# A memset between two scatters of GpSimd, one word wide or 320 columns on all partitions

## The chip, the cores and the metric

The kernel runs on one core of a Trainium2 chip. The core has five engines that work side by side, each in the order of its own instructions: PE (matrix products), DVE (VectorE), ACT (ScalarE), POOL (GpSimd) and SP (which here only issues transfers). They wait for one another through semaphores. The metric is device time in microseconds. Before the change it is 736.45 us, the median of three runs (736.4 to 737.74).

## The reference

The input x holds 64 sequences of 128 tokens with 128 features, the context 64 sequences of 77 tokens with 96 features. A gated cross-attention with 16 heads is followed by a gated mixture of 8 experts, of which each token takes its two best:

```python
x = x + tanh(g_xattn[0]) * xattn(layernorm(x), ctx_768, mask, Wq, Wk, Wv, Wo)
x = x + tanh(g_ffn[0]) * ffn(layernorm(x), Wg, W11, W12, W2)
# xattn: softmax(q k^T * 8**-0.5) v per head, then Wo
# ffn:   top 2 of softmax(x Wg), scores divided by their sum;
#        per expert (silu(x W11) * (x W12)) W2; weighted sum of the two
```

The reference computes all experts for all tokens and then picks. The kernel sends each token only to its two experts.

## The kernel before

The 64 sequences are worked in 16 groups of four (G = 4). The kernel has three stages.

**Attention and gating** (lines 268 to 758). One loop runs over the 64 sequences. In turn i it computes the scores of sequence i, transposes and exponentiates those of i-1 and mixes the values of i-2. The work that belongs to a whole group is cut into small functions, each registered with `step(dt)`: the function runs for group g in turn 4g + dt, after the turn's attention (or ahead of it, with PRE). `advance` (line 731) calls what is due, over the groups in order. So turn i carries steps of several groups, and steps whose numbers differ by four fall into the same turn. The order on PE, ACT, DVE and POOL is exactly the order in which the code issues instructions (`manual_schedule`, line 279): no engine overtakes its own queue. Steps reach up to 30, so the loop goes on for some 25 turns after the attention of the last sequence.

The steps that matter here use POOL. The first layer norm has its factors on POOL (`factors`, lines 305 to 311, in steps -13), and so has the selection matrix `sel` (steps -14 to -12). After the attention of a group, the second layer norm has its factors on POOL (step 13). The token numbers are written by an iota (line 497, step 15), the normed rows are copied a second time (line 506, step 16), the chosen experts are turned into one-hot form (`took`, lines 555 to 569, step 22), and the counts per expert are kept up (`both` and `run`, lines 573 to 578, step 23). PE turns the counts into places (`pp`, lines 584 and 585, step 24), POOL picks the places (`at`, line 597, step 25), DVE sums them (`to`, line 604) and POOL casts them to integers (`dest`, line 606, step 26).

Then the tokens are dispatched. Steps 27 to 30 call `dispatch(b)` for the four sequences of the group. Each issues two indirect transfers from the queue of POOL, which write the 128 rows of a sequence (132 words each) to the places of their first and second expert in the DRAM buffer `xg`. After each of them POOL clears the tile `spare_w`:

```python
i = nc.gpsimd.indirect_dma_start(
    out=xg[:, :],
    out_offset=bass.IndirectOffsetOnAxis(ap=gr.dest[:, k, b : b + 1], axis=0),
    in_=gr.rows[:, b, k, :], in_offset=None,
)
apart(i, "dispatch")
nc.gpsimd.memset(spare_w, 0.0)
```

Nothing reads `spare_w`. There are 64 x 2 = 128 scatters and as many memsets. The scatters are declared to touch rows of their own, so they don't wait for one another.

**Expert tiles** (lines 761 to 898). The counts give a table of 135 tiles of 128 rows (lines 766 to 803). SP fills the unused rows with empty ones (lines 805 to 812) and loads one tile after another (`load`, line 831), which needs all scatters to have landed. PE multiplies with the expert's weights (lines 851 and 874), and POOL scatters each result to `yb` (line 881).

**Sum** (lines 901 to 919). The two results of each token are loaded, weighted, added to x and stored.

Of the kernel before, what the change touches and what calls it, by code (L numbers as in the profile page):

```python
# [8 lines left out]
F32 = mybir.dt.float32  # L9
# [25 lines left out]
def tile_gated_xattn_moe(  # L35
# [21 lines left out]
    P = 128  # L57
# [14 lines left out]
    const = ctx.enter_context(tc.tile_pool(name="const", bufs=1))  # L72
# [181 lines left out]
    czs = [const.tile([CD, G, 3, JL], F32, name=f"czs{i}") for i in range(3)]  # L254
    for t in pls + czs:
        nc.gpsimd.memset(t, 0.0)
    spare_w = const.tile([1, 1], F32, name="spare_w")

    wt = keep.tile([P, NG, G, TOPK], F32, name="wt")

# [692 lines left out]
```

## Time and profile before

| what | us |
|---|---|
| median of three runs | 736.45 |
| profiled execution, its own time | 771.93 |
| its span | 770.0 |
| POOL busy in the span | 420.9 |
| scatters of the tokens, L611, 128 of them | 129.2 |
| memsets of `spare_w`, L620, 128 of them | 11.3 |
| first and last scatter of the tokens start at | 166.4 and 489.9 |
| attention, one group before and after the scatters begin | 21.3 and 26.1 |
| expert tiles, from about 501 to 723 | 222 |

The profile shows one execution, taken by the hardware profiler, and it took longer than the runs without it. Its parts are the busy time of each engine, the same over 40 slices of the span, the chain of work that ended last, and groups of instructions by line. In a group's row stand the line, the engine, the operation, what it writes and reads, how often, then the busy time in us, the mean of one in ns, and the idle time of the engine ahead of it with what ended that idle time. A timeline row begins with start and length in us; the value in brackets is the idle time ahead, with what ended it. A row of waits gives total, number of times and longest. "issue" is time in which an engine waited for nothing that the profile shows.

### The profile page before, as it was taken

The numbers are of one execution on the slowest core, as the hardware profiler recorded it, in microseconds if no ns is written. First come the engines' busy times: TensorE is split into PE (matmuls) and PEld (weight loads), VectorE is DVE, ScalarE is ACT, GpSimd is POOL, SyncE is SP. The second block draws the span as 40 slices with busy tenths as digits, with TensorE's granted clock in tenths as the row PEclk, the third lists the DMA queues.
The fourth block names the chain that finished last, engine by engine and source line by source line (L and its number), as shares of the span: only waits on it lengthen the run. The fifth ranks groups of instructions, "written<-read, shape, count | busy, mean of one in ns | idle before, by whom it ended". The sixth has DMA issues, their size and how long they took to land.

```text
span 770.0 us, 21086 instructions
## 1 busy us (share of the span) xinstructions
PE 610.8 (79%) x7626; PEld 439.4 (57%) x7626; DVE 473.5 (61%) x1446; ACT 363.9 (47%) x881; POOL 420.9 (55%) x792
## 2 busy tenths in 40 slices
PE   2999999999999889999983220299999999999400
PEld 1677777776676666776762120166666666666300
DVE  4567888987677777677864113155544554555297
ACT  1678787776666666677542100043443344434100
POOL 5411133356767676755668888445665556555400
PEclk9999999999999999999995555599999999999755
DMA  6841111111211111011112011222222222222299
GB/s 184 212 118 30 29 29 29 23 22 43 50 43 32 38 38 38 25 39 46 39 46 49 32 39 60 70 63 82 81 82 82 80 81 83 75 84 81 65 323 289
DMA packets 86948, 56.86 MB, mean 74 GB/s; under 512 B 15773, under 2 KB 82738, under 8 KB 86848
## 3 DMA queue, kind: packets, MB, share of 16 engines
q1 hardware_dynamic: 68512, 33.78, 18.7%
q0 software_dynamic: 8416, 17.06, 6.7%
q10 hardware_dynamic: 9920, 4.69, 2.1%
q8 instruction: 62, 1.02, 0.5%
q14 instruction: 38, 0.31, 0.1%
HBM read 28.50 MB, written 22.73 MB: 67 GB/s over the span
## 4 chain that ended last, share of the span: by engine, by line
PE 68%; POOL 11%; ACT 6%; issue 5%; DMA 4%; DVE 3%; SPq 1%; POOLq 0%; ACTq 0%; DVEq 0%
PE pu L851 14%; PE po L717 13%; PE pot L874 7%; PE tp L685 7%; POOL xg L611 7%; PE sc L663 5%; PE phh L866 4%; PE tl L698 3%; PE pv L638 2%; DVE x L913 2%; ACT kb L421 2%; DMA ys<-yb 2%; PE pq L432 2%; PE ptt L841 2%; PE py L470 2%
## 5 line engine op out<-in xcount | busy, mean ns | idle before, releaser
L881 POOL DMA_INDIRECT yb<-y,xt x135 | 132.6, 982 | 102.2 <-DVE xTt L843 83.8
L611 POOL DMA_INDIRECT xg<-rows,dest x128 | 129.2, 1010 | 24.9 <-issue 24.9
L851 PE MATMUL pu<-wx,xTt 128*128 x270 | 140.3, 601 | 0.8 <-DVE xTt L843 0.5
L672 DVE TENSOR_REDUCE mx<-sc 128x16 f32<-128x1232 f32 x64 | 92.3, 1442 | 66.2 <-PE sc L663 65.2
L859 DVE TENSOR_TENSOR ht<-sgt,pu 128x256 f32<-128x256 f32 x135 | 56.8, 421 | 96.1 <-issue 80.7
L857 ACT ACTIVATE sgt<-pu 128x256 f32<-128x256 f32 x135 | 51.8, 384 | 130.1 <-PE pu L851 96.4
L690 ACT ACTIVATE pT<-tp,drop 128x512 f32<-128x512 f32 x128 | 81.9, 688 | 42.2 <-PE tp L685 41.2
L874 PE MATMUL pot<-wx,hTt 128*128 x540 | 82.4, 275 | 0.1
L675 DVE TENSOR_TENSOR pe<-sc,mx 128x1024 f32<-128x1024 f32 x64 | 78.4, 1224 | 2.2
L866 PEld LDWEIGHTS phh<-ident,ht 128*128 128x128 f32 x270 | 38.0, 141 | 70.1 <-issue 67.4
L874 PEld LDWEIGHTS pot<-wx,hTt 128*128 128x128 f32 x540 | 70.8, 191 | 0.5 <-DVE y L880 0.3
L685 PEld LDWEIGHTS tp<-ident,pe 128*128 128x128 f32 x512 | 55.5, 142 | 26.8 <-issue 14.7
L685 PE MATMUL tp<-ident,pe 128*128 128x128 f32 x512 | 70.8, 282 | 0.0
L717 PE MATMUL po<-pT,va 128*32 128x128 f32 x1536 | 64.5, 275 | 6.8 <-issue 4.3
L717 PE MATMUL po<-pT,own 128*32 128x128 f32 x1536 | 65.1, 273 | 5.0 <-issue 4.8
L654 ACT COPY va<-pv 128x384 f32<-128x384 f32 x64 | 30.8, 481 | 52.7 <-PE po L717 40.2
L841 PE MATMUL ptt<-ident,xt 128*128 128x128 f32 x135 | 37.5, 278 | 22.4 <-DMA xt<-xg 22.0
L717 PEld LDWEIGHTS po<-pT,own 128*32 128x32 f32 x1536 | 47.7, 110 | 10.8 <-issue 10.4
L663 PE MATMUL sc<-kb,qT 32*128 32x308 f32 x512 | 52.5, 480 | 0.0
L866 PE MATMUL phh<-ident,ht 128*128 128x128 f32 x270 | 51.6, 273 | 0.0
L717 PEld LDWEIGHTS po<-pT,va 128*32 128x32 f32 x1536 | 41.5, 110 | 15.4 <-issue 11.7
L868 ACT COPY hTt<-phh 128x256 f32<-128x256 f32 x135 | 49.5, 368 | 1.4 <-PE pot L874 0.7
(158 smaller groups left out, 1063.8 us busy)
## 6 DMA issues: line engine op xcount, KB each, us to landing
xt<-xg SPq DMA_DIRECT2D x135, 66.0 KB
ys<-yb SPq DMA_DIRECT2D x32, 256.0 KB
rb<-rz SPq DMA_DIRECT2D x64, 64.0 KB
out_dram<-x ACTq DMA_DIRECT2D x16, 256.0 KB
x<-in_x_dram SPq DMA_DIRECT2D x15, 256.0 KB
yb<-y,xt POOLq DMA_INDIRECT x135
wx<-in_L_ffn_W_dram SPq DMA_DIRECT2D x2, 1024.0 KB
xg<-rows,dest POOLq DMA_INDIRECT x128
```

Source lines behind the costliest of these rows:

```text
L611: i = nc.gpsimd.indirect_dma_start(out=xg[:, :], out_offset=bass.IndirectOffsetOnAxis(ap=gr.dest[:, k, b : b + 1], axis=0), in_=gr.rows[:, ...
L663: nc.tensor.matmul(sc[:, q, :W], gr.qT[r, b * S : (b + 1) * S], gr.kb[r, b].rearrange("p h j -> p (h j)"), start=True, stop=True,)
L672: nc.vector.tensor_reduce(mx[:, :, :, 0], sv, AX.X, ALU.max)
L675: nc.vector.tensor_tensor(dst[:, :, :, : j1 - j0], sv[:, :, :, j0:j1], mx.to_broadcast([P, NQ, HQ, j1 - j0]), ALU.subtract,)
L685: nc.tensor.transpose(tp[:, u, :], pe[:, q + u // 2, 2 * (u % 2) : 2 * (u % 2) + 2].rearrange("p h j -> p (h j)"), ident,)
L690: nc.scalar.activation(pT[:, 2 * q : 2 * q + 4], tp, AF.Exp, bias=drop[:, 0, i : i + 1], scale=scale)
L717: nc.tensor.matmul(po[32 * q : 32 * q + 32, v, :], w, pT[:, 2 * q + c if c < 2 else 8 + q // 2, :], start=(c == 0), stop=(c == 2),)
L851: nc.tensor.matmul(pu.rearrange("p j i -> p (j i)"), ti.xT, wxf[:, bass.ds(ti.e, 2 * I)], start=True, stop=True,)
L859: nc.vector.tensor_tensor(ti.h.rearrange("p c i -> p (c i)"), sg, pu[:, 1], ALU.mult)
L866: nc.tensor.transpose(pt[:, c], ti.h[:, c], ident)
L874: nc.tensor.matmul(po, ti.hT[:, c], wxf[:, bass.ds(ti.e + w, D)], start=(c == 0), stop=(c == NC - 1),)
L881: i = nc.gpsimd.indirect_dma_start(out=yb[:, :], out_offset=bass.IndirectOffsetOnAxis(ap=ti.x[:, D : D + 1].bitcast(I32), axis=0), in_=y, ...
```

## The change

The tile `spare_w` gets 320 columns on all 128 partitions, where it was one word on one partition. The memset in `dispatch` is written for the whole tile, so it now fills 128 x 320 words each of its 128 times. Order, waits and transfers are as they were.

```diff
-    spare_w = const.tile([1, 1], F32, name="spare_w")
+    spare_w = const.tile([P, 320], F32, name="spare_w")
```

## The prediction

> **What bounds the kernel now.** I read the page's busy table and slices first. No engine bounds the whole span, so it has to be cut into stages.
>
> ```profile
> PE 610.8 (79%) x7626; PEld 439.4 (57%) x7626; DVE 473.5 (61%) x1446; ACT 363.9 (47%) x881; POOL 420.9 (55%) x792
> ...
> PE   2999999999999889999983220299999999999400
> ...
> POOL 5411133356767676755668888445665556555400
> ```
>
> The reader is to see the dip of PE to 2 or 3 tenths in the slices from 400 to 490 us, where POOL stands at 8. I cut the span there and asked for the stages: one group of the attention with scatters running, the dip, and the expert tiles (columns: stage, length, then busy time and count of PE, PEld, DVE, ACT, POOL).
>
> ```profile
> 269.00:295.00 26.00, 23.76 (x401) 17.38 (x401) 19.50 (x56) 16.91 (x39) 17.81 (x40) 1.00 0.15 35
> 399.20:491.00 91.80, 20.05 (x102) 16.83 (x94) 26.26 (x144) 8.57 (x21) 78.31 (x183) 0.53 0.16 47
> 501.00:723.00 222.00, 219.53 (x1207) 148.69 (x1206) 111.40 (x402) 87.42 (x269) 130.39 (x133) 1.00 0.27 78
> ```
>
> The expert stage belongs to PE (219.5 of 222) and has no spare_w memset. In the dip POOL is busy 78.3 of 91.8 us, and nearly all the rest is the 10.4 us marked "issue" ahead of its 52 scatters plus gaps below 0.2 us. The waits of that stage say who is late:
>
> ```profile
> PEld pp L584 <- POOL both L575: 42.0, 4, 12.1
> POOL rows L506 <- ACT rows L321: 2.7, 1, 2.7
> ```
>
> POOL waits for another engine once, at 399.1, and after that the others wait for it. The chain that ended last runs over POOL from 399.14 to the last scatter (489.95), then its landing (2.34), SP's loads of xt and the first expert tile. So what POOL does between 399 and 490 sets the end.
>
> Then the POOL timeline within the dip and, in a second fence, the rows of the memsets (groups by shape: busy, mean ns, idle before):
>
> ```profile
> 427.04 0.09 POOL L620 MEMSET spare_w<- 1x1 f32 x1
> 427.10 0.25 POOL L575 TENSOR_TENSOR both<-took 128x32 f32<-128x32 f32 x1
> 427.43 1.03 POOL L578 TENSOR_TENSOR run<-run,both 128x8 f32<-128x8 f32 x4
> 428.41 0.27 POOL L497 IOTA rows<- 128x16 int32 x2
> 428.84 0.98 POOL L611 DMA_INDIRECT xg<-rows,dest  x1 [0.16 <-issue]
> 429.83 0.09 POOL L620 MEMSET spare_w<- 1x1 f32 x1
> 430.13 0.97 POOL L611 DMA_INDIRECT xg<-rows,dest  x1 [0.21 <-issue]
> ```
>
> ```profile
> L620 POOL MEMSET spare_w<- 1x1 f32 x128 | 11.3, 88 | 0.3
> L256 POOL MEMSET pls<- 128x256 f32 x3 | 0.8, 301 | 0.0
> L256 POOL MEMSET czs<- 96x192 f32 x3 | 0.6, 248 | 0.0
> ```
>
> POOL's instructions follow one another here without waiting for anyone.
>
> [...] from 192 to 256 columns 301 - 248 = 53 ns, 0.83 ns a column. [...] Spacing here confirms the slope: three memsets of 256 columns take 0.76 us (4.09 to 4.85), three of 192 take 0.60 (4.85 to 5.45), so 0.253 and 0.200 each, again 0.83 ns a column. [...]
>
> **The change part by part.** Nothing is removed, added or moved: 128 memsets keep their places and their waits, and each writes 320 columns of 128 partitions in place of one word. Price: 88 ns now; 301 + 64 x 0.83 = 354 ns after. That is 266 ns more, and 319 x 0.83 = 265 by the spacing. Can this hide in the gap ahead of the next scatter? From the predecessor's end to the scatter's end it takes 0.21 + 0.96 = 1.17 us after today's memset, 1.14 after the iota (428.68 to 429.82), 1.16 after the copy L506 (0.61 long). The length of the predecessor adds in full, and at most 0.03 of the gap goes. I take 0.01 off for the 31 memsets or so of the dip that stand directly before a scatter.
>
> *In the dip*: 52 memsets start from 401.2 to 490.9. The last has no scatter behind it, so 51 count: 51 x 0.266 = 13.6, less 31 x 0.01 = 0.3, gives 13.3 us on the path. Bounds: 12.6 if 0.03 goes each time, 13.6 if nothing goes.
>
> *Before the dip*: 76 memsets, 20.2 us of POOL work. What hides it is POOL's idle time, here in the group at 269 us:
>
> ```profile
> 275.38 0.24 POOL L307 TENSOR_SCALAR ve_a<-mv_a 128x4 f32<-128x4 f32 x1 [0.87 <-DVE mv_a L303]
> ...
> 282.80 0.61 POOL L506 COPY rows<-rows 128x512 f32<-128x512 f32 x1 [2.37 <-ACT rows L321]
> ...
> 287.66 0.69 POOL L307 TENSOR_SCALAR ve_f<-mv_f 128x4 f32<-128x4 f32 x1 [0.76 <-DVE mv_f L303]
> ...
> 293.57 0.19 POOL L606 CAST dest<-to 128x8 int32<-128x8 f32 x1 [1.44 <-DVE to L604]
> ```
>
> There are four steps to a group, two memsets to a step (0.53 us), and each step ends in a wait of at least 0.76, so POOL arrives later and still waits. One step, at 382.43, has only 0.38; 0.15 us carries over into the next wait of 0.79, which still leaves 0.11. Queued behind the memsets are both and run (PE's pp L584 waits for them), at (VectorE's to L604), and the rest of the next scatter. They come 0.3 to 0.5 us later; both ends at 348.03 where pp starts at 354.88, so about 6.9 us lie between. Cost: nothing, and the 20.2 us in full if that cover is gone. The ready counts let SP's empty rows go out well before the last scatter, which stays so.
>
> Everything behind the last scatter moves by the same amount: landing, loads, expert tiles, sum. The tile takes 1276 bytes more of each partition; I set this to nothing.
>
> Sum for the profiled execution: 771.93 + 13.3 = 785.2 (span 770.0 to 783.3). The median of the runs is 736.45, 35.5 us below its own profile, and I add the same 13.3 there: **749.8 us**, +1.8%. The dip consists of POOL's own work and its memsets are fixed by the order of steps, so I expect its share to be alike in both. What may differ is the cover: a group takes 21.3 us before the scatters start and 26.1 after (six groups, 4.8 x 6 = 29 us), and if the unprofiled runs lack that stretching, POOL's spare 5.9 us a group fall to 1.1 while the memsets ask for 2.1. That leaves it 1.0 us late per group, 6 us in all by 321 us. Behind that, POOL has 5 to 7 us idle in each group of this trace and can catch up, and pp's 6.9 us of slack takes such a lag. So 0 to 6 us may come on top, up to 756.
>
> **The rivals.**
> *The cover fails.* POOL becomes the bound already in the attention. For it: the 35.5 us above. Against: the four waits shown. In part, 752 to 757; in full, 736.45 + 13.3 + 20.2 = 770.
> *Part is absorbed.* [...] less than the 0.266 counts. Half gives 743. [...] Against: iota and copy add in full.
> *Not slower.* The scatter's 0.96 us could hold a wait [...], and a longer memset would stand in that wait. It decides if that wait is 0.266 or more in every scatter of the dip; then the time stays at 736.5. For: three scatters of the dip take 1.24, 1.31 and 1.65 us, together 1.3 us above the usual. Against: the expert stage's scatters (L881), with 0.6 us of idle ahead of each, take 982 ns, no less than the 960 of two scatters that stand close. Shorter than before would need the three outliers and more.
>
> **How the numbers follow.** The dip alone (748 to 751.5): 0.63. Some of the attention as well (751.5 to 757): 0.17; beyond 757: 0.06. Partly absorbed (738 to 748): 0.10. Not slower: 0.04. About 0.2% (1.5 us) is what a measurement of this kernel can tell from no change. The range 746 to 757 holds the first two and a little of the absorbed case, some 0.82. Faster 0.02, same 0.03, slower 0.95.
>
> **What would show it.** The row of L620 at about 354 ns x128; POOL's stretch from the last wait for ACT to the last scatter at some 104 us in place of 90.8; 52 memsets still in it; groups at 26 us as before; POOL's four waits per group shorter by about half a microsecond each; expert stage 222 us. Wrong if the groups of the attention grow (the cover), if scatters behind the memset get shorter (the absorbed wait), or if L620 reads well off 354 ns.

## The result and the profile after

The changed kernel takes 750.58 us (median of four runs, 750.0 to 751.12), the kernel before 736.42 beside it (four runs, 736.13 to 737.74). The ratio is 1.0181, with a 95% interval from 1.0162 to 1.0200: 14.2 us or 1.8% slower, against 13.3 us predicted.

One thing has to be said first, or the two profiles contradict each other. The profiled execution of the changed kernel has a span of 749.1 us and fits its runs. The one shown of the kernel before had 770.0 us, 35 more than the runs of that kernel. A repeat of the kernel before (run e0 below) left a profile with a span of 734.9 us, and all comparisons here are with that one. The experiments ran on three chips. On that of e0 to e3 the kernel before takes 737 us; on that of e4 to e8 and on that of e9 and ea it takes 772 us in every run. So the first profile shows something real, only not what the timed runs did.

The stages of the changed kernel: one group of the attention with scatters, the stretch from POOL's 13th copy of rows to the last scatter, and the expert tiles (columns as before: stage, length, busy time of PE, PEld, DVE, ACT, POOL, then clock and DMA).

```profile
229.50:251.22 21.72, 21.53 (x401) 16.75 (x402) 19.18 (x56) 16.83 (x39) 19.51 (x41) 1.00 0.18 42
366.29:470.12 103.83, 19.06 (x82) 16.28 (x82) 26.23 (x143) 7.71 (x20) 91.89 (x183) 0.52 0.14 41
481.00:702.30 221.30, 218.99 (x1206) 148.67 (x1206) 110.27 (x402) 87.21 (x269) 130.59 (x133) 1.00 0.29 78
```

The same three stages in the repeat of the kernel before:

```profile
228.60:250.30 21.70, 21.50 (x400) 16.61 (x400) 18.93 (x52) 16.56 (x38) 17.63 (x38) 1.00 0.18 42
365.07:455.68 90.61, 20.01 (x102) 16.79 (x90) 26.19 (x143) 8.57 (x21) 77.12 (x182) 0.53 0.16 48
466.50:688.00 221.50, 219.60 (x1208) 148.51 (x1206) 110.38 (x402) 87.61 (x270) 130.66 (x133) 1.00 0.27 78
```

A group of the attention lasts the same 21.7 us in both, with POOL busy 19.5 instead of 17.6 us. The expert stage hasn't moved. The middle stage is 13.2 us longer. In it POOL waits for no other engine; the rows of its waits in the changed kernel, from 348.6 us on, are:

```profile
POOL xg L611 <- issue: 9.9, 59, 0.2
POOL xg L611 <- POOL dest L606: 0.3, 1, 0.3
```

The rows of the memset and of the scatters in the changed kernel (groups by shape; one line's instructions with shortest, median and longest in ns, and the first and last start):

```profile
L620 POOL MEMSET spare_w<- 128x320 f32 x128 | 49.1, 384 | 0.3
```

```profile
L611 POOL DMA_INDIRECT xg<-rows,dest x128: 964/980/1433, 166.4 to 470.1; - x128
```

And the scatters of the repeat of the kernel before:

```profile
L611 POOL DMA_INDIRECT xg<-rows,dest x128: 954/973/1646, 165.9 to 455.7; - x128
```

A scatter takes as long as it did, 980 ns in the median against 973. The last one starts 14.4 us later, and the span is 14.2 us longer: all of the loss lies ahead of the last scatter.

How the memset stands among its neighbours is seen in the timeline of POOL. First the changed kernel:

```profile
245.07 0.97 POOL L611 DMA_INDIRECT xg<-rows,dest  x1 [0.17 <-issue]
246.03 0.39 POOL L620 MEMSET spare_w<- 128x320 f32 x1
246.36 0.33 POOL L597 TENSOR_TENSOR at<-took,place 128x64 f32<-128x64 f32 x1
```

Then the same place in the repeat of the kernel before:

```profile
265.51 0.97 POOL L611 DMA_INDIRECT xg<-rows,dest  x1 [0.21 <-issue]
266.47 0.09 POOL L620 MEMSET spare_w<- 1x1 f32 x1
266.52 0.34 POOL L597 TENSOR_TENSOR at<-took,place 128x64 f32<-128x64 f32 x1
267.41 0.69 POOL L307 TENSOR_SCALAR ve_f<-mv_f 128x4 f32<-128x4 f32 x1 [0.55 <-DVE mv_f L303]
```

The memset's row reads 384 - 88 = 296 ns more. But from its start to the start of `at` it is 0.33 against 0.05 us, so 0.28 more; and where a scatter follows, from the memset's start to the scatter's end, it is 1.52 (244.52 to 246.04) against 1.27 (265.21 to 266.48), so 0.25 more, because the gap ahead of the scatter shrinks from 0.21 to 0.17. The mean of the two is the 0.265 of 319 columns, and the middle stage is longer by 13.2 us for 51 memsets, 0.259 each. So the spacing tells what a memset cost here, and the 296 ns of its row are too many.

### The profile page after: what moved, and what is told of

Same layout as the page of the kernel before. It is cut to its first block, busy times and chain, and to the rows that moved or that the text cites. A ratio compares the mean times of both kernels' runs of the same rounds, so it can differ in the third digit from the quotient of the medians.

```text
span 749.1 us, 21086 instructions
## 1 busy us (share of the span) xinstructions
PE 592.0 (79%) x7626; PEld 434.4 (58%) x7626; DVE 470.5 (63%) x1446; ACT 362.6 (48%) x881; POOL 454.0 (61%) x792
## 4 chain that ended last, share of the span: by engine, by line
PE 68%; POOL 15%; ACT 5%; issue 4%; DVE 3%; DMA 3%; SPq 1%; POOLq 0%; ACTq 0%; DVEq 0%
PE pu L851 15%; PE po L717 11%; POOL xg L611 8%; PE pot L874 8%; PE tp L685 7%; PE sc L663 5%; PE phh L866 4%; DVE x L913 3%; POOL spare_w L620 3%; PE pv L638 3%; PE tl L698 2%; PE pq L432 2%; ACT kb L421 2%; PE ptt L841 2%; PE pv L648 2%
## 5 line engine op out<-in xcount | busy, mean ns | idle before, releaser
L611 POOL DMA_INDIRECT xg<-rows,dest x128 | 129.4, 1011 | 21.7 <-issue 21.4
L717 PE MATMUL po<-pT,va 128*32 128x128 f32 x1536 | 54.2, 274 | 2.0 <-ACT kb L421 1.5
L584 PE MATMUL pp<-both,earlier 128*128 128x32 f32 x32 | 6.6, 290 | 61.4 <-POOL both L575 61.4
L717 PE MATMUL po<-pT,own 128*32 128x128 f32 x1536 | 53.7, 273 | 0.0
L620 POOL MEMSET spare_w<- 128x320 f32 x128 | 49.1, 384 | 0.3
L843 DVE COPY xTt<-ptt 128x128 f32<-128x128 f32 x135 | 37.9, 281 | 16.2 <-PE ptt L841 16.2
```

The source lines that it names most:

```text
L611: i = nc.gpsimd.indirect_dma_start(out=xg[:, :], out_offset=bass.IndirectOffsetOnAxis(ap=gr.dest[:, k, b : b + 1], axis=0), in_=gr.rows[:, ...
L717: nc.tensor.matmul(po[32 * q : 32 * q + 32, v, :], w, pT[:, 2 * q + c if c < 2 else 8 + q // 2, :], start=(c == 0), stop=(c == 2),)
```

## The experiments

**e0, the kernel before once more.** No edit.

> The kernel before, unchanged, for a profile of an execution that takes what the runs take. Both theories: 736.4 us, ratio 1.000. If the profiled execution shown ahead of the prediction (771.9 us) was stretched in the attention, then here a group with scatters takes about 21.7 us as it does in the changed kernel's profile, not 26.1, and POOL is idle about 2 us in a group (21.7 less the some 19.6 us of its own work). The dip from the last wait of POOL to the last scatter should then start with 52 to 60 scatters still to come, and the last scatter should start at about 456 us. If instead the stretching lies elsewhere, the groups stay at 26.

Measured: 736.93 us, ratio 1.0002 (0.9995 to 1.0009). The groups last 21.7 us. POOL's waits in one group:

```profile
250.31 0.19 POOL L606 CAST dest<-to 128x8 int32<-128x8 f32 x1 [0.19 <-DVE to L604]
250.86 0.19 POOL L556 CAST ki<-i 128x8 f32<-128x8 uint32 x1 [0.35 <-DVE gt L551]
...
257.74 0.24 POOL L307 TENSOR_SCALAR ve_a<-mv_a 128x4 f32<-128x4 f32 x1 [0.45 <-DVE mv_a L303]
```

With the 0.55 at 267.41 above that is 1.5 us in a group, and one of the four waits of the first profile, that for the rows, is gone until 306 us. The eight memsets of a group ask for 2.1 us. So in an execution that takes what the timed ones take, the recorded waits are too short to cover them. The last scatter starts at 455.7, as expected.

**e1 and e2, one half each.** A second tile keeps the one-word memset:

```diff
-                    nc.gpsimd.memset(spare_w, 0.0)
+                    nc.gpsimd.memset(spare_w if G * g + 27 + b >= 65 else spare_n, 0.0)  # e1
+                    nc.gpsimd.memset(spare_n if G * g + 27 + b >= 65 else spare_w, 0.0)  # e2
```

> The 320-column memset only in the scatter steps that fall after the last attention turn (52 of the 128), one word in the others. Theory (only the memsets that POOL runs with no wait left count): nearly the whole loss, +13.3 us, 749.7. Rival (the cover in the attention fails as well and the loss is spread over all 128): 52/128 of 14.2, +5.8 us, 742.2.

> The other half: 320 columns in the first 76 memsets, one word in the 52 after the attention. Theory: POOL's waits hide them, +0 to 2 us, 736.4 to 738.4. Rival (spread evenly): +8.4 us, 744.8. POOL's idle time in a group should be close to zero here, and the last scatter should start where it does in the kernel before, or up to 2 us later.

Measured: e1 750.45 us, 13.4 more than the 737.04 of the kernel before beside it (ratio 1.0183, 1.0157 to 1.0210); e2 738.14, 1.1 more (1.0019, 1.0009 to 1.0028). The two add up to the 14.2 of the whole change, within their intervals. Fewer than half of the memsets carry over nine tenths of the cost. An even spread is refuted twice, by 5.8 against 13.4 and by 8.4 against 1.1. The last scatters confirm it; first e1, then e2:

```profile
L612 POOL DMA_INDIRECT xg<-rows,dest x128: 954/976/1430, 166.3 to 468.7; - x128
```

```profile
L612 POOL DMA_INDIRECT xg<-rows,dest x128: 954/980/1645, 165.8 to 456.7; - x128
```

**e3 and e4, other widths.** The tile is `[P, 640]` and `[P, 160]`.

> 640 columns in all 128 memsets: 0.267 us more on each than in the changed kernel. Theory: in the changed kernel's profile POOL hardly waits any more in the attention, so the second 320 columns are hidden nowhere: 127 x 0.267 = 33.9 us on top of 750.6, 784.5, and less than that only by the some 4 us that POOL still waits. Rival (cover as good as for the first 320): 14.2 more, 764.8.

> 160 columns in all 128 memsets. Theory (0.83 ns a column, only the memsets after the attention count): 159 x 0.83 = 0.132 us each, 51 of them 6.7 us, and in the attention POOL's waits hide 8 x 0.132 = 1.1 us a group altogether: 737.0 + 6.7 = 743.7. Rival (a fixed price for a memset that is not a single word): the same 13.5 as with 320 columns, 750.5.

Measured: e3 778.42 us, 41.4 more than before (ratio 1.0556, 1.0527 to 1.0585), so 27.2 on top of the first 14.2. The direction is the theory's: the second 320 columns cost almost twice as much as the first. The size is 6 us short of 784.5. The expectation set the waits left in the changed kernel at some 4 us; counted afterwards, from the first scatter to 348.6 us in its profile, they are 5.7 for the rows and 1.1 for ve_f, 6.9 in all, and 33.9 - 6.9 = 27.0. In e3 the attention itself has become longer, 24.3 us a group (the casts of `dest` start at 236.78 and 261.05), and PE waits for `both` there (2.1 us in four waits from 190 to 330 us).

e4 ran on the second chip, where the kernel before takes 772.28 beside it: 777.63, ratio 1.0088 (1.0060 to 1.0115). That is 6.8 us by the ratio and 5.4 by the medians, where the theory had 6.7. A fixed price for any memset beyond a word would have given 13.5, which lies outside the interval (4.6 to 8.9). The rows of the two widths, e3 and then e4:

```profile
L620 POOL MEMSET spare_w<- 128x640 f32 x128 | 83.3, 650 | 0.3
```

```profile
L620 POOL MEMSET spare_w<- 128x160 f32 x128 | 32.1, 251 | 0.3
```

From 160 to 640 columns the row grows by 399 ns, 0.83 a column.

**e6 and e7, what of the fill costs.** In e6 the tile is `[1, 320]`; in e7 it is `[P, 320]`, but the memset fills `spare_w[:1, :1]`. Both ran on the second chip, too, beside 772.28 us.

> The memset fills 320 columns of one partition only. Theory (the columns cost[...]): as 128 partitions, 750.5. Rival (the number of words [...] costs): close to the kernel before, 737 to 738.

> The tile is 128 x 320, but the memset fills one word of it. Separates the fill from the 1276 bytes a partition by which the later tiles move. Theory: 737.0, ratio 1.000. Rival (the moved tiles cost or gain): anything beyond 1.5 us.

Measured: e6 ratio 1.0170 (1.0136 to 1.0203), 13.1 us more by the ratio; e7 ratio 0.9995 (0.9981 to 1.0009). The large tile costs nothing that can be measured. 320 words in one partition cost as much as 40,960 words in all, within the intervals (13.1 us against 14.2), so in these runs columns are what is paid for. The row of e6:

```profile
L620 POOL MEMSET spare_w<- 1x320 f32 x128 | 45.3, 354 | 0.2
```

354 ns is the price that the prediction had worked out for 320 columns. What refutes the rival by which only part of that price counts is the middle stage above, where 51 memsets take 13.2 us more, 0.259 each.

**ea, the changed kernel beside the kernel before on the third chip.** No edit.

> The changed kernel again, beside the other. On a chip where the kernel before takes about 772 us, its groups with scatters take 26 us and POOL waits 5.9 us in each, so the attention should hide its share in full: +13.2 us, ratio 1.017. On one where it takes about 737 us, POOL waits only some 1.7 us a group: +14.4 us, ratio 1.019 to 1.020. Rival (no difference between the two in what is hidden): 14.2 us on either.

Measured: 783.77 against 771.79, ratio 1.0147 (1.0104 to 1.0190), 11.3 us by the ratio and 12.0 by the medians. The interval reaches from 8 to 15 us and so holds 13.2 as well as 14.2: it doesn't tell the two apart. The price of the stretch after the attention is the same there: from the 13th copy of rows (397.06 us) to the last scatter (501.24) it is 104.2 us, against 90.8 in the first profile of the kernel before (399.14 to 489.95).

**e8 and e9, a kernel in which POOL has less to do after the attention.** In the steps that fall into turn 65 or later, `ki`, `took`, `gt`, `wt`, `both`, `run`, `at`, `dest` and the second copy of the rows move to VectorE:

```diff
+        def free(g, dt):
+            return nc.vector if G * g + dt >= 65 else nc.gpsimd
...
-                nc.gpsimd.tensor_tensor(run[:, i + 1], run[:, i], gr.both[:, b], ALU.add)
+                free(g, 23).tensor_tensor(run[:, i + 1], run[:, i], gr.both[:, b], ALU.add)
```

(the others alike). e8 keeps the one-word memset, e9 has 128 x 320.

> Starts from the kernel before, one-word memset. In the steps that fall after the last attention turn (turn 65 on) the small operations took, gt, wt, both, run, at, dest and the second copy of the rows move from POOL to VectorE, which is idle there for some 70% of the time; POOL keeps the scatters, the memsets, the iotas and the factors of the norm. Theory (POOL's own work after the attention sets the end): in the repeat of the kernel before, POOL takes 90.6 us from its last wait to the last scatter; 52 scatters with their memsets at 1.24 us make 64.5, the factors and iotas some 6, so up to 20 us go: 717 to 722. Rival (the chain of counts and places through PE and VectorE sets the end as soon as POOL is faster): half of it or less, 727 to 735.

> The kernel in which VectorE takes POOL's small work after the attention, now with the 320-column memset. There the chain that ended last ran over SP's writes of empty rows and no longer over POOL. Theory (a memset counts only from where POOL is late): 51 x 0.26 = 13.3 us less the some 3.5 us by which POOL is early there, so about 10 us more than with one word, ratio to the kernel before about 0.983 + 0.013 = 0.996. Rival (the price of a memset counts wherever it stands): 13.3 to 14.2 more, ratio 1.001 to 1.002.

Measured: e8 758.17 against 772.28, ratio 0.9833 (0.9803 to 0.9864): faster than the kernel before on the second chip by 12.9 us by the ratio, 14.1 by the medians. Both forecasts missed: it is less than the theory's 15 to 20 us and more than the rival's half. The timeline of POOL in e8 shows what is left:

```profile
430.13 0.96 POOL L614 DMA_INDIRECT xg<-rows,dest  x1 [0.21 <-issue]
431.08 0.09 POOL L623 MEMSET spare_w<- 1x1 f32 x1
431.39 0.96 POOL L614 DMA_INDIRECT xg<-rows,dest  x1 [0.23 <-issue]
432.34 0.09 POOL L623 MEMSET spare_w<- 1x1 f32 x1
432.39 0.29 POOL L500 IOTA rows<- 128x16 int32 x2
```

Two scatters with a memset between follow one another after 1.26 us. From the 13th copy of rows (398.87) to the last scatter (471.81) it is 72.9 us, 17.9 less than in the first profile. Some 3.6 us are given back behind it: 755.5 - 471.8 = 283.7 us to the end, against 770.0 - 489.9 = 280.1. The chain that ended last explains that. It can be followed back to 473.4 us, and from there on it runs over SP and holds no scatter:

```profile
473.45 0.70 issue
474.14 0.70 SPq L812
474.84 0.01 issue
474.86 0.69 SPq L812
...
476.76 1.61 DMA xg<-empty
```

The last of SP's writes of empty rows starts at 476.76, after the last scatter, and SP's loads begin when it has landed (478.4). So in e8 these writes end the stage. But there SP is also slow: from the landing that it last waited for (473.44) to the start of the last write it takes 3.3 us, where eight of these writes take 8.7 us in the first profile (474.23 to 482.90), 1.1 each. Why it is slow there was not found.

e9, on the third chip: 770.09 against 771.79, ratio 0.9973 (0.9953 to 0.9994). From 0.9833 to 0.9973 is 0.0140 of 772, 10.8 us, as the theory had it. That agreement is luck, since its mechanism is not in the profile. In e9 the chain that ended last runs over POOL's scatters and memsets from 445.29 us to the last memset (483.49) and holds no write of empty rows, so POOL isn't early against these. And a second thing changed beside the memset. The iota `tn` (line 790), for which the table of expert tiles on VectorE waits, stands outside the part with a fixed order. In all other timelines 24 scatters are still to come behind it (it starts at 440.20 in e8); in e9 it stands behind them all. POOL, then VectorE:

```profile
482.52 0.96 POOL L614 DMA_INDIRECT xg<-rows,dest  x1 [0.17 <-issue]
483.49 0.38 POOL L623 MEMSET spare_w<- 128x320 f32 x1
483.81 0.28 POOL L790 IOTA tn<- 128x135 f32 x1
```

```profile
484.12 1.28 DVE L795 TENSOR_TENSOR ge__7381<-tn,after 128x1080 f32<-128x1080 f32 x1 [35.05 <-POOL tn L790]
```

The table is ready only at 490.6, and SP's loads of tiles begin behind it, at 490.59. From the last scatter to the end it is 769.5 - 482.5 = 287.0 us, against 283.7 in e8 and 279.3 in e7 (769.5 - 490.2). The last scatter itself starts 10.7 us after that of e8. So e8 and e9 don't measure what the wide memset costs where something else is later than POOL. They ran on different chips besides, and the two intervals together leave some 8 to 13.6 us for the difference, which holds the rival's 13.3. The theory's claim stays unproven.

## Why the prediction was right, and where not

**The price of a memset**: predicted 266 ns, less 10 before a scatter. Right by the spacing (0.25 and 0.28). The prediction also said that the row would read 354. It reads 384, and exactly 354 with one partition (e6). The rows of 128-partition memsets in the scatter steps lie 30 ns above what the memsets at the kernel's start gave. Little of that shows in the spacing: from the start of a memset to the end of the scatter behind it the median after the attention is 1.51 us in the changed kernel and 1.27 in the repeat, 0.24 more.

**51 memsets in the dip, 13.3 us**: right, and for the reason given. 103.8 - 90.6 = 13.2 in the profiles, and 13.4 in e1. The larger tile at nothing was right as well (e7).

**76 memsets before the dip at nothing**: wrong by 1.1 us, and for a reason that the prediction had seen from far off. It read the cover from an execution whose groups took 26.1 us, with waits of at least 0.76 at four places of a group. In the repeat, which takes what the timed runs take, a group takes 21.7 us and POOL's waits in it come to 1.5 to 1.7. So the argument of the four waits failed, and the prediction's second case (groups at 21.3, 1.1 us of spare, 0 to 6 us on top) was the true one, at its lower end.

That it came out at the lower end is in part luck. The memsets of a group ask for 2.1 us and the waits hold 1.6, but a row changed too: `ve_f` takes 0.69 us where it has waited and 0.23 to 0.26 where it hasn't, but for one case with 0.69 and no recorded wait (351.91 in the changed kernel). The next row starts that much sooner. Why the row changes was not found. Here first the repeat of the kernel before, then the changed kernel:

```profile
223.74 0.69 POOL L307 TENSOR_SCALAR ve_f<-mv_f 128x4 f32<-128x4 f32 x1 [0.63 <-DVE mv_f L303]
```

```profile
224.94 0.23 POOL L307 TENSOR_SCALAR ve_f<-mv_f 128x4 f32<-128x4 f32 x1
```

1.6 and 0.46 make the 2.1 us. From 176.66 to 285.46 us, five groups, POOL in the changed kernel doesn't wait for another engine even once, and each group still takes 21.7 to 21.8 us. The cover was used up to the last, and the prediction had not counted on that row.

The group ahead of these five is 0.8 us longer than before, which goes into the wait of the 10th copy of rows. From there on POOL waits for the rows again, and the 12th copy of rows starts at 347.96 before and 347.93 after. The loss arises in the eight memsets between that copy and the 13th, 17.1 us before and 18.4 after. The halves agree: it is 17.1 in e1 and 18.4 in e2. The views of the place:

The repeat of the kernel before:

```profile
347.96 0.61 POOL L506 COPY rows<-rows 128x512 f32<-128x512 f32 x1 [2.52 <-ACT rows L321]
...
351.94 0.70 POOL L307 TENSOR_SCALAR ve_f<-mv_f 128x4 f32<-128x4 f32 x1 [0.56 <-DVE mv_f L303]
...
365.07 0.61 POOL L506 COPY rows<-rows 128x512 f32<-128x512 f32 x1 [0.30 <-ACT rows L321]
```

The changed kernel:

```profile
347.93 0.61 POOL L506 COPY rows<-rows 128x512 f32<-128x512 f32 x1 [1.43 <-ACT rows L321]
...
366.29 0.97 POOL L506 COPY rows<-rows 128x512 f32<-128x512 f32 x1
```

Eight memsets ask for 2.1 us, and the two waits between hold 0.86; the rest is the 1.25 us. The prediction had marked this place as the thinnest (a wait of 0.38 with 0.11 left over behind it), but in the stretched execution it just held.

**The rivals.** Cover failing in full (770): refuted by e2, but e3 shows where it begins, since at 640 columns the attention pays too. Part absorbed: refuted by the 13.2 us of the dip and by e1 (13.4); e4 and e6 agree (6.8 and 13.1 by the ratio). Not slower, if a scatter's row held a wait that a longer memset would fill: refuted, as its median is 973 ns before and 980 after. Of the long scatters of the dip (1.30 and 1.65 us in the repeat) one stays (1.43), which is worth about half a microsecond.

**What was to be seen**: the stretch at some 104 us (103.8), the expert stage unmoved (221.3). "Groups at 26 as before" held only in so far as they are as before; they are at 21.7. POOL's waits in a group, which were to be shorter by half a microsecond each, are gone altogether in five groups.

Left open: how the 1.1 us would stand on the chips with 772 us, where POOL has more spare time in the attention (5.8 us of recorded waits in a group of e7, 205.44 to 231.43 us, against 1.5 in the repeat). ea doesn't resolve it.

## What to carry to other kernels

Here an instruction that "does nothing" cost its time where its engine ran without a wait (13.4 us for the memsets after the attention, e1), so count the instances in that stretch and multiply by the spacing. The others were nearly free (1.1 us, e2) until the cover was used up, and then they cost as well, as most of the second 320 columns did (27.2 of 33.9 us, e3). The cover is not only the waits that a profile records: a row that waited can itself be longer, as `ve_f` was by 0.46 us here. Before reading small covers of half a microsecond off a profile, compare the profiled execution's own time with the runs: here they differed by 5%, and the waits in it were not those of the timed runs. Where one engine drains a queue alone while another idles, moving small work across can be worth as much as trimming the fill (e8, 12.9 us). And before two runs are compared, look whether the edit moved something else, as it moved `tn` in e9.

## What was not expected of the hardware

The same program takes 737 us on one chip (734.8 to 739.0 in 39 runs) and 772 on two others (769.2 to 774.9 in 24 runs, 770.2 to 773.8 in 15). The runs of each chip lie close together in time, so that it is the chip that makes the difference isn't shown. The difference lies in the attention while scatters run, and for the most part in the products of the mixing: both halves of them, with the idle time ahead of them, account for 28 of the 35 us between the two profiles below. The row of half of these products in the repeat of the kernel before, on the first chip:

```profile
L717 PE MATMUL po<-pT,own 128*32 128x128 f32 x1536 | 53.7, 273 | 0.0
```

The same in e7, on the second chip:

```profile
L717 PE MATMUL po<-pT,own 128*32 128x128 f32 x1536 | 64.2, 274 | 4.5 <-issue 4.4
```

Each product is as long, 273 and 274 ns, but they overlap less (1536 of them keep PE busy for 53.7 and 64.2 us), and PE stands idle for 4.4 us with nothing that the profile shows it to wait for. The granted clock doesn't account for it: over the attention with scatters it is 0.98 in e7 (164 to 396 us) against 1.00 in the repeat, but from 190 to 242 us of e7 it is 1.00, and the group in that stretch (205.44 to 231.43 us) takes 26.0 us. Before the scatters begin a group takes 21.3 us on both (132.06 to 153.39 in the repeat, 132.27 to 153.59 in e7). What holds PE's issue back was not found. And a scatter of 128 rows with a one-word memset between comes 1.26 us after the one before it in e8 (430.13 to 431.39), of which 0.96 is its own row and 0.21 to 0.23 a gap. Behind the memset of 320 columns the gap is 0.17 in the changed kernel, and behind the iota 0.16 in the first profile: a longer instruction ahead took no more than some 0.05 off it.
